# Two-layer graph network, residual and layer norm on one core: merged sums written into the PSUM tile of the sums, in pairs in the first layer

## The chip, the cores and the metric

One of the eight cores of a Trainium2 chip runs the kernel. The time is device microseconds of one execution. Four runs of the kernel before gave 2027.91, 2038.23, 2041.61 and 2043.71 us, median 2039.92 us.

## What is computed

`x` has 6250 rows (nodes) of 256 numbers. 100,000 edges go from `src` to `dst`; they are sorted by `dst`, and low-numbered nodes have many more incoming edges than high-numbered ones. In all shapes float32:

```
def _gin_agg(h, src, dst, eps, n_nodes):
    agg = jax.ops.segment_sum(h[src], dst, num_segments=n_nodes)
    return (1.0 + eps) * h + agg
...
    h = _gin_agg(x, src, dst, eps1, n)
    h = jax.nn.relu(h @ W1a + b1a)
    h = jax.nn.relu(h @ W1b + b1b)
    h = _gin_agg(h, src, dst, eps2, n)
    h = jax.nn.relu(h @ W2a + b2a)
    out = h @ W2b + b2b
...
    x = _layernorm(x + _L0_gnn_ref(x, edge_index, ...), axis=-1)
```

W1a is 256x512, W1b and W2a 512x512, W2b 512x256. So layer 1 sums rows of 256 numbers, layer 2 rows of 512.

## The kernel before, in words

The 100,000 edges make 782 chunks of 128. The first 216 chunks end at the 512 lowest nodes (the "heavy" ones); their sums are not gathered, but computed as products of a matrix of counts with all of `x` (or of the hidden `h`): 52 products a layer (line 648), added to the accumulators on VectorE (line 654). In layer 1 the counts must first be made (lines 700 to 759: VectorE's vectors `ca` and `cb`, a matmul on line 747, a copy on ScalarE, an add on VectorE).

The other 566 chunks are gathered. They fall into 94 groups of 20 to 4 chunks; the last 62 groups have 4. GpSimd issues one indirect transfer a chunk (line 505) into tiles of four chunks ("pieces"), six pieces ahead. For each group, in this order:

1. VectorE makes a selection matrix `sel` of 0 and 1 (line 517, two buffers) and a matrix `to` (line 522, three buffers) two groups ahead.
2. TensorE sums the gathered rows by 32 slots (line 854): the chunks of a group go to four parts of 32 partitions of one PSUM tile `pm`.
3. ScalarE copies `pm` to `split` in SBUF (line 872).
4. TensorE multiplies `split` by `to`, which brings the four parts' slots to their place among 128 nodes (line 877, the "unite"), into another PSUM tile `pu`.
5. VectorE adds `pu` times a mask to 3 or 4 accumulator tiles of 128 nodes (line 881).

When all adds to four accumulator tiles are done, that block of 512 nodes goes through the dense layers: transposes (line 576), two matrix products (lines 588 and 599), with copies and activations on ScalarE and VectorE. The four buffers of accumulators (line 484) are loaded on SP's queue (line 487) and scaled on ScalarE five chunks later (line 494).

The order of the instructions on each engine is written out by the loop at the end of `layer` (line 832 on); an engine works strictly in that order and waits where a value is missing. The loop issues a piece's four chunks of sums, then counts `now` up four times. At each count it issues what is due (`due`, line 533), and gives two queues a chance (`pump`): `blockwise`, the dense blocks that are ready, and `beside`, the counts and products, which earns credit at a rate set by a planner. Two queue steps or none may come between two due items. Due times: the copy comes `LAG` = 2 chunks after the group's end, the unite 1 chunk after the copy, the adds 2 after the unite.

PSUM has eight banks. Three hold the dense steps, two the counts of layer 1, and `SUMS` (3 in layer 1, 5 in layer 2) are shared by `pm`, `pu` and the products' tiles. `sum_tile` (line 547) hands them out: when all are taken, the oldest's due work is issued at once. A tile of 128x256 float32 fills half a bank, one of 128x512 a whole one.

The functions that the change touches:

Of the kernel before, what the change touches and what calls it, by code (L numbers as in the profile page):

```python
# [15 lines left out]
P = 128  # L16
# [11 lines left out]
STEP2 = 1.5  # L28
ACCS = 4
LAG = 2  # L30
SPREAD = 5.0
# [90 lines left out]
def tile_gin_residual_layernorm(  # L122
# [64 lines left out]
    srcs = const.tile([P, NCP], I32, name="srcs")  # L187
    dsti = const.tile([P, NCP], I32, name="dsti")
    dstf = const.tile([P, NCP], F32, name="dstf")
    slot = const.tile([P, NCP], F32, name="slot")  # L190
    nc.gpsimd.memset(srcs, 0)
    nc.gpsimd.memset(dsti, 0)

# [35 lines left out]
    with tc.tile_pool(name="prep", bufs=2) as prep, tc.tile_pool(  # L229
        name="prepp", bufs=2, space=bass.MemoryType.PSUM  # L230
    ) as prepp:
        full = E // P
        rest = E - full * P
# [187 lines left out]
    def ordered(ctx):  # L421
# [14 lines left out]
        for g in order:  # L436
            m = members[g]
            pieces += [(g, m[i : i + BURST]) for i in range(0, len(m), BURST)]
        first_use, last_use = {}, {}
        for k, g in enumerate(order):  # L440
# [16 lines left out]
        def layer(number, ctx, table, width, scale, wa, ba, wb, wide, prepare, finish, conclude):  # L457
# [4 lines left out]
                tc.tile_pool(name=f"psum{number}", bufs=2, space=bass.MemoryType.PSUM)  # L462
            )
            SUMS = 3 if number == 1 else 5
            acc = {}
            held = []
# [12 lines left out]
            def seed(ts):  # L479
                while len(held) >= ACCS:  # L480
                    assert blockwise.todo
                    blockwise.step()
# [30 lines left out]
            def select(g):  # L513
                c0, h = groups[g]
                n = min(PARTS * h, NCH - c0)
                sel = edge.tile([P, GRP, SLOTS], F32, tag="sel", name="sel", bufs=2)
                nc.vector.tensor_tensor(  # L517
                    sel[:, :n, :], iota[:, :SLOTS].unsqueeze(1).to_broadcast([P, n, SLOTS]),
                    slot[:, c0 : c0 + n].unsqueeze(2).to_broadcast([P, n, SLOTS]), op=ALU.is_equal,
                )  # L520
                to = edge.tile([P, P], F32, tag="to", name="to")
                nc.vector.tensor_scalar(to, iota, home[:, g : g + 1], None, op0=ALU.is_equal)  # L522
                sels[g] = sel, to
# [23 lines left out]
            def sum_tile(name):  # L547
                while len(sums_out) >= SUMS:
                    take(sums_out[0])
                pm = psum.tile([P, width], F32, tag="pm", name=name, bufs=SUMS)  # L550
                entry = [pm, None]
                sums_out.append(entry)
                return entry

            def take(entry):
                if entry in sums_out:
                    sums_out.remove(entry)
                    entry[1]()

            def take_later(entry, what):  # L560
                entry[1] = what
                later(LAG, lambda: take(entry))

# [46 lines left out]
            def products(turns, table_of):  # L610
# [28 lines left out]
                for i, (r, t) in enumerate(turns):  # L639
# [4 lines left out]
                    entry = sum_tile("pm")  # L644
                    pm = entry[0]
                    for j, k in enumerate(ks):
# [9 lines left out]

                    take_later(entry, add_product)
                    yield 0.00167 * len(ks) * width
# [126 lines left out]
            class Queue:  # L785
# [15 lines left out]
                def pump(self):  # L801
                    self.credit = min(self.credit + self.rate, 4.0)
                    if self.credit > 0:
                        self.step()

            unseeded = [b for b in blocks if b[0] >= HEAVY]
            waiting = list(blocks)
# [24 lines left out]
            for k, g in enumerate(order):  # L832
# [13 lines left out]
                beside.rate = rates[g]  # L846
                entry = sum_tile("pm")
                pm = entry[0]
                sel, to = sels.pop(g)
                parts = [[c for c, b in members[g] if b == i] for i in range(PARTS)]  # L850
                while upto < len(pieces) and pieces[upto][0] == g:
                    rows_, reads = gathered.pop(upto)
                    for j, (c, b) in enumerate(pieces[upto][1]):
                        mm = nc.tensor.matmul(  # L854
                            pm[b * SLOTS : (b + 1) * SLOTS], sel[:, c - c0, :], rows_[:, j, :],
                            start=(c == parts[b][0]), stop=(c == parts[b][-1]),
# [10 lines left out]

                def add_group(g=g, pm=pm, to=to, parts=parts):

                    split = edge.tile([P, width], F32, tag="split", name="split", bufs=2)  # L870
                    used = SLOTS * sum(1 for p in parts if p)
                    nc.scalar.copy(split[:used], pm[:used])  # L872

                    def unite():
                        entry = sum_tile("pu")
                        pu = entry[0]
                        nc.tensor.matmul(pu, to[:used], split[:used], start=True, stop=True)  # L877

                        def add():
                            for t in range(lo[g], min(hi[g], NT - 1) + 1):  # L880
                                nc.vector.scalar_tensor_tensor(  # L881
                                    acc[t], pu, mask[:, t - lo[g], g : g + 1], acc[t],
                                    op0=ALU.mult, op1=ALU.add,
                                )
# [333 lines left out]
```

## Time and profile before

| | |
|---|---|
| median of 4 runs | 2039.92 us (2027.91 to 2043.71) |
| the profiled execution | 2041.31 us |
| its span, first to last instruction | 2039.4 us |
| TensorE clock granted, mean | 0.853 of full |
| layer 1 / layer 2 in the span, about | 45 to 1007 us / 1022 to 2030 us |
| TensorE (PE) busy | 1414.3 us, 69% |
| GpSimd (POOL) busy | 1090.5 us, 53% |
| VectorE (DVE) busy | 823.0 us, 40% |
| ScalarE (ACT) busy | 372.1 us, 18% |
| DMA, mean | 165 GB/s |

How to read the profile: it shows one execution. PE is the matmuls, PEld the weight loads that run beside them. A float32 matmul appears as two rows. A group is all instructions of one line, engine and operation; `pu<-split,to` means that the tile `pu` is written from `split` and `to`. Behind `x` stands the number of instructions, behind the first bar the busy us and the mean ns of one, behind the second the idle time of the engine just before them and what ended most of it. A line of the waits has the engine, its tile and line, what it waited for, total us, times and the longest. A timeline row has the start and length in us, and in brackets the idle time before it. "issue" and "remote" say that the profile found no instruction that ended the wait.

### The profile page before, as it was taken

The page shows a single profiled execution, that of the slowest core. Times are in us where ns is not written, and L with a number is a line of the kernel's source. Part 1 is how long each engine was busy: PE and PEld are TensorE (multiplying, and loading weights), DVE is VectorE, ACT ScalarE, POOL GpSimd, SP SyncE. Part 2 cuts the span into 40 slices and gives each one's busy share as a digit, 9 for nine tenths or more (in the row PEclk, how much of TensorE's full clock was granted, in tenths as well). Part 3 has the DMA queues.
Part 4 walks back from the last instruction along what each step waited for, and adds up shares of the span by engine and source line. Part 5 has one row for each costly group of instructions (what it writes and reads, how often), then busy time and mean ns, then how long its engine had stood idle before and what let it go on. Part 6 is the DMA issues. An engine that isn't in the chain of part 4 may idle for free.

```text
span 2039.4 us, 17219 instructions
## 1 busy us (share of the span) xinstructions
PE 1414.3 (69%) x5364; PEld 622.0 (30%) x5364; DVE 823.0 (40%) x2253; ACT 372.1 (18%) x683; POOL 1090.5 (53%) x1146
## 2 busy tenths in 40 slices
PE   1244475676867867887675679585959677878777
PEld 0011132332434434433321223231314323334334
DVE  7255544444444434333211223233425366446534
ACT  0022222322222221221200001010111111111111
POOL 2766666656564465444066665646465465445420
PEclk9966687977978888997887779788969889989989
DMA  5332345545445456432297776757576486456521
GB/s 162 90 94 86 91 141 170 176 127 181 152 144 183 141 184 213 133 106 80 69 329 222 250 227 213 249 153 261 162 247 196 131 265 197 137 173 192 164 86 38
DMA packets 157811, 337.08 MB, mean 165 GB/s; under 512 B 23954, under 2 KB 70930, under 8 KB 157712
## 3 DMA queue, kind: packets, MB, share of 16 engines
q0 software_dynamic: 72448, 222.63, 36.0%
q1 hardware_dynamic: 74756, 96.90, 14.0%
q10 hardware_dynamic: 10508, 16.35, 2.3%
q8 instruction: 47, 0.77, 0.1%
q14 instruction: 52, 0.43, 0.1%
HBM read 303.75 MB, written 32.05 MB: 165 GB/s over the span
## 4 chain that ended last, share of the span: by engine, by line
PE 39%; issue 23%; another core or an unknown queue 13%; POOL 8%; DVE 6%; DMA 6%; ACT 3%; SPq 1%; DVEq 0%; ACTq 0%; POOLq 0%
PE po L599 10%; PE ph L588 10%; POOL g L505 8%; PE pm L648 8%; PE pm L854 6%; PE pu L877 3%; DVE acc L881 3%; DMA r<-in_x_dram 2%; DMA acc<-h 2%; PE pt L576 1%; PE pc L747 1%; DMA g<-h,srcs 1%; ACT split L872 1%; DMA g<-in_x_dram,srcs 1%
## 5 line engine op out<-in xcount | busy, mean ns | idle before, releaser
L505 POOL DMA_INDIRECT g<-h,srcs x566 | 537.0, 949 | 473.0 <-issue 216.6
L505 POOL DMA_INDIRECT g<-in_x_dram,srcs x566 | 550.0, 972 | 370.3 <-issue 149.0
L881 DVE SCALAR_TENSOR_TENSOR acc<-pu,mask,acc 128x256 f32<-128x256 f32 (+1 forms) x666 | 365.1, 607 | 103.4 <-PE pu L877 47.0
L877 PE MATMUL pu<-split,to 128*128 128x256 f32 (+2 forms) x376 | 192.3, 598 | 220.9 <-ACT split L872 146.1
L648 PE MATMUL pm<-xr,cf 128*128 128x256 f32 (+3 forms) x784 | 308.8, 541 | 49.3 <-issue 29.9
L854 PE MATMUL pm<-g,sel 128*32 128x256 f32 (+1 forms) x2264 | 279.5, 561 | 81.3 <-issue 31.1
L648 PEld LDWEIGHTS pm<-xr,cf 128*128 128x128 f32 (+1 forms) x784 | 164.4, 217 | 208.5 <-issue 160.8
L654 DVE TENSOR_TENSOR acc<-pm,acc 128x256 f32<-128x256 f32 (+1 forms) x104 | 57.7, 555 | 410.0 <-remote 198.8
L747 PE MATMUL pc<-cb,ca 128*128 128x490 f16 x216 | 89.1, 485 | 146.7 <-DVE cb L708 37.3
L588 PE MATMUL ph<-zt,w2a_s 128*128 128x512 f32 (+1 forms) x416 | 184.1, 596 | 5.2 <-ACT zt L579 5.2
L599 PE MATMUL po<-w1b_s,ht 128*128 128x512 f32 (+1 forms) x392 | 174.0, 595 | 0.0
L877 PEld LDWEIGHTS pu<-split,to 128*128 128x128 f32 (+1 forms) x376 | 71.4, 219 | 321.6 <-ACT split L872 178.9
L872 ACT COPY split<-pm 128x256 f32<-128x256 f32 (+2 forms) x188 | 88.1, 479 | 394.4 <-remote 209.6
L854 PEld LDWEIGHTS pm<-g,sel 128*32 128x32 f32 x2264 | 51.7, 116 | 284.4 <-issue 225.1
L738 ACT CAST cs<-pc 128x490 f16<-128x490 f32 x151 | 84.5, 570 | 245.3 <-remote 129.3
L517 DVE TENSOR_TENSOR sel<-iota,slot 128x128 f32<-128x128 f32 (+5 forms) x188 | 65.5, 349 | 137.0 <-remote 78.3
L588 PE MATMUL ph<-zt,w1a_s 128*128 128x512 f32 (+1 forms) x208 | 105.9, 648 | 21.5 <-issue 12.0
L588 PEld LDWEIGHTS ph<-zt,w2a_s 128*128 128x128 f32 x416 | 79.4, 203 | 112.7 <-issue 89.0
L704 DVE TENSOR_SCALAR ca<-wide,low 128x128 f16<-128x128 f16 x216 | 59.5, 275 | 125.6 <-remote 79.1
L522 DVE TENSOR_SCALAR to<-iota,home 128x128 f32<-128x128 f32 x188 | 57.4, 305 | 111.4 <-PE pu L877 64.9
L576 PE MATMUL pt<-ident,acc 128*128 128x128 f32 (+1 forms) x294 | 56.5, 335 | 65.5 <-issue 51.2
L599 PEld LDWEIGHTS po<-w1b_s,ht 128*128 128x128 f32 (+1 forms) x392 | 73.4, 189 | 88.0 <-issue 86.7
(104 smaller groups left out, 828.6 us busy)
## 6 DMA issues: line engine op xcount, KB each, us to landing
xr<-in_x_dram SPq DMA_DIRECT2D x48, 512.0 KB
h<-h1r ACTq DMA_DIRECT2D x48, 256.0 KB
counts<-cf SPq DMA_DIRECT2D x48, 256.0 KB
acc<-h SPq DMA_DIRECT2D x12, 1024.0 KB
xr<-h SPq DMA_DIRECT2D x12, 1024.0 KB
cf<-counts SPq DMA_DIRECT2D x48, 256.0 KB
g<-in_x_dram,srcs POOLq DMA_INDIRECT x566
g<-h,srcs POOLq DMA_INDIRECT x566
```

Of the source, the lines that this page charges most:

```text
L505: nc.gpsimd.indirect_dma_start(out=tile_[:, j, :], out_offset=None, in_=table, in_offset=bass.IndirectOffsetOnAxis(ap=srcs[:, c : c + 1], ...
L517: nc.vector.tensor_tensor(sel[:, :n, :], iota[:, :SLOTS].unsqueeze(1).to_broadcast([P, n, SLOTS]), slot[:, c0 : c0 + n].unsqueeze(2).to_br ...
L576: nc.tensor.transpose(pt[:, k, :m], a[:m, k * P : (k + 1) * P], ident[:m, :m])
L588: nc.tensor.matmul(ph[:, :nb], wa[:, k, f * P : (f + 1) * P], zt[:, k, :nb], start=(k == 0), stop=(k == kk - 1),)
L599: nc.tensor.matmul(po[:m], ht[:, f, i * P : i * P + m], wb[:, f, :], start=(f == 0), stop=(f == KH - 1),)
L648: nc.tensor.matmul(pm, cf[:m, j, :], xr[:m, j, :], start=(j == 0), stop=(j == len(ks) - 1),)
L738: nc.scalar.copy(cs, pc)
L747: mm = nc.tensor.matmul(pc, a, b, start=(i == 0), stop=(i == len(pair) - 1))
L854: mm = nc.tensor.matmul(pm[b * SLOTS : (b + 1) * SLOTS], sel[:, c - c0, :], rows_[:, j, :], start=(c == parts[b][0]), stop=(c == parts[b][ ...
L872: nc.scalar.copy(split[:used], pm[:used])
L877: nc.tensor.matmul(pu, to[:used], split[:used], start=True, stop=True)
L881: nc.vector.scalar_tensor_tensor(acc[t], pu, mask[:, t - lo[g], g : g + 1], acc[t], op0=ALU.mult, op1=ALU.add,)
```

## The change

`pu` is gone: the unite writes into the tile that held the group's sums. In layer 1 two groups share a tile (`BATCH` = 512 // width = 2), so one copy serves two groups; layer 2 keeps one group a tile. The copy, the unites and the adds of a tile are a list, taken one after the other, each two chunks after the one before (`LAGS`). A tile is given back after its last list entry. `to` gets six buffers. `dsti`, needed only at the start, moves to a pool that is closed after it. The last group always has a tile of its own. In `seed`, what is due is issued if no dense step is left to do.

```diff
+LAGS = (2, 2, 2)
...
-    dsti = const.tile([P, NCP], I32, name="dsti")
...
-    nc.gpsimd.memset(dsti, 0)
...
+        dsti = prep.tile([P, NCP], I32, tag="dsti", name="dsti", bufs=1)
+        nc.gpsimd.memset(dsti, 0)
...
+        def batched(n):
+
+            rest = order[:-1]
+            return [rest[i : i + n] for i in range(0, len(rest), n)] + [order[-1:]]
+
...
+            BATCH = 512 // width
             SUMS = 3 if number == 1 else 5
+            batch_of = {g: b for b in batched(BATCH) for g in b}
...
                 while len(held) >= ACCS:
+                    if not blockwise.todo:
+                        due(all=True)
                     assert blockwise.todo
                     blockwise.step()
...
-                to = edge.tile([P, P], F32, tag="to", name="to")
+                to = edge.tile([P, P], F32, tag="to", name="to", bufs=6)
...
             def sum_tile(name):
                 while len(sums_out) >= SUMS:
-                    take(sums_out[0])
-                pm = psum.tile([P, width], F32, tag="pm", name=name, bufs=SUMS)
-                entry = [pm, None]
+                    oldest = sums_out[0]
+                    assert oldest[1]
+                    while oldest[1]:
+                        take(oldest, len(oldest[1]))
+                pm = psum.tile([P, BATCH, width], F32, tag="pm", name=name, bufs=SUMS)
+                entry = [pm, []]
                 sums_out.append(entry)
                 return entry
 
-            def take(entry):
-                if entry in sums_out:
-                    sums_out.remove(entry)
-                    entry[1]()
-
-            def take_later(entry, what):
-                entry[1] = what
-                later(LAG, lambda: take(entry))
+            def take(entry, left_over):
+
+                if len(entry[1]) == left_over:
+                    entry[1].pop(0)[1]()
+                    if entry[1]:
+                        take_later(entry)
+                    else:
+                        sums_out.remove(entry)
+
+            def take_later(entry):
+                n = len(entry[1])
+                later(entry[1][0][0], lambda: take(entry, n))
...
-                    take_later(entry, add_product)
+                    entry[1].append((LAG, add_product))
+                    take_later(entry)
...
+            def add_batch(pm, of):
+
+                n = len(of)
+                used = max(u for g, to, u in of)
+                split = None
+
+                def copy():
+                    nonlocal split
+                    split = edge.tile([P, BATCH, width], F32, tag="split", name="split", bufs=2)
+                    nc.scalar.copy(split[:used, :n, :], pm[:used, :n, :])
+
+                def unite():
+                    for i, (g, to, u) in enumerate(of):
+                        nc.tensor.matmul(pm[:, i, :], to[:u], split[:u, i, :], start=True, stop=True)
+
+                def add():
+                    for i, (g, to, u) in enumerate(of):
+                        for t in range(lo[g], min(hi[g], NT - 1) + 1):
+                            nc.vector.scalar_tensor_tensor(
+                                acc[t], pm[:, i, :], mask[:, t - lo[g], g : g + 1], acc[t],
+                                op0=ALU.mult, op1=ALU.add,
+                            )
+                            uses[t] -= 1
+
+                return list(zip(LAGS, (copy, unite, add)))
...
-                entry = sum_tile("pm")
+                batch = batch_of[g]
+                if g == batch[0]:
+                    entry = sum_tile("pm")
+                    members_to = []
                 pm = entry[0]
+                at = batch.index(g)
...
-                            pm[b * SLOTS : (b + 1) * SLOTS], sel[:, c - c0, :], rows_[:, j, :],
+                            pm[b * SLOTS : (b + 1) * SLOTS, at, :],
+                            sel[:, c - c0, :], rows_[:, j, :],
...
-                def add_group(g=g, pm=pm, to=to, parts=parts):
-
-                    split = edge.tile([P, width], F32, tag="split", name="split", bufs=2)
-                    used = SLOTS * sum(1 for p in parts if p)
-                    nc.scalar.copy(split[:used], pm[:used])
-
-                    def unite():
-                        entry = sum_tile("pu")
-                        pu = entry[0]
-                        nc.tensor.matmul(pu, to[:used], split[:used], start=True, stop=True)
-
-                        def add():
-                            for t in range(lo[g], min(hi[g], NT - 1) + 1):
-                                nc.vector.scalar_tensor_tensor(
-                                    acc[t], pu, mask[:, t - lo[g], g : g + 1], acc[t],
-                                    op0=ALU.mult, op1=ALU.add,
-                                )
-                                uses[t] -= 1
-
-                        take_later(entry, add)
-
-                    later(1, unite)
-
-                take_later(entry, add_group)
+                members_to.append((g, to, SLOTS * sum(1 for p in parts if p)))
+                if g == batch[-1]:
+                    entry[1] += add_batch(pm, members_to)
+                    take_later(entry)
```

More of the change, by code (lines that the diff above doesn't have):

```diff
@@ L644, in products @@
                     entry = sum_tile("pm")
-                    pm = entry[0]
+                    pm = entry[0][:, 0, :]
                     for j, k in enumerate(ks):
```

## The prediction, made before the changed kernel was run

> **What bounds the kernel now.** I read the busy times first, then the waits of TensorE and of GpSimd, then the groups by shape, then the timeline where the waits are long.
>
> ```profile
> PE 1414.3 (69%) x5364; PEld 622.0 (30%) x5364; DVE 823.0 (40%) x2253; ACT 372.1 (18%) x683; POOL 1090.5 (53%) x1146
> ```
>
> No engine is full. PE has the most work and is idle for 2039.4 - 1414.3 = 625 us. GpSimd, which issues the gathers, comes second, so its waits say who leads:
>
> ```profile
> POOL g L505 <- issue: 365.7, 968, 68.2
> POOL g L505 <- PE pm L854: 303.8, 62, 11.6
> ```
>
> The columns are total us, times, longest. 62 long waits end when PE has used up a gathered tile: gathers run ahead of PE, six pieces deep, and stop for PE. So PE's chain sets the pace, and what counts is what PE stands idle for:
>
> ```profile
> PE pu L877 <- ACT split L872: 146.1, 40, 22.4
> PE pm L648 <- DVE acc L881: 13.2, 10, 3.6
> PE pm L854 <- ACT split L872: 9.1, 2, 7.1
> ```
>
> The largest single entry is the merging matmul (the "unite" on line 877) waiting for ScalarE's copy of the sums. The groups by shape give all idle time before it, whatever the releaser (the number behind the second bar):
>
> ```profile
> L877 PE MATMUL pu<-split,to 128*128 128x512 f32 x186 | 115.8, 709 | 152.0 <-ACT split L872 97.4 <-issue 27.2 <-ACT acc L494 15.4
> L877 PE MATMUL pu<-split,to 128*128 128x256 f32 x186 | 74.6, 489 | 66.9 <-ACT split L872 46.6 <-issue 10.7 <-DVE acc L881 5.2
> ```
>
> So 66.9 us in layer 1 (width 256), 152.0 us in layer 2 (width 512), 1.9 us more for the two short last groups: 220.9 us, a third of PE's idle time. This is what the change is aimed at.
>
> But not all of it is the copy. Going through the timeline unite by unite, 21 of the 188 stand over 3 us and hold 160.6 us (8 with 40.1 us in layer 1, 13 with 120.5 us in layer 2); the copy itself takes 0.373 us (128x256) or 0.585 us (128x512). The timeline shows what a long stop is made of:
>
> ```profile
> 639.89 1.99 PE L648 MATMUL pm<-xr,cf 128*128 128x256 f32 x8 [0.58 <-DVE acc L881]
> ...
> 644.83 0.29 DVE L517 TENSOR_TENSOR sel<-iota,slot 128x128 f32<-128x128 f32 x1 [4.14 <-remote]
> 644.89 0.37 ACT L872 COPY split<-pm 128x256 f32<-128x256 f32 x1 [3.88 <-remote]
> ...
> 645.31 0.64 PE L854 MATMUL pm<-g,sel 128*32 128x256 f32 x8 [3.43 <-issue]
> ```
>
> PE's last product is over at 641.9 by its row, yet VectorE's next selection and ScalarE's copy, both readers of sums that PE made before 641.9, start together at 644.8. They got PE's signal late, and PE then waited for them. In such a stop every reader of PE waits, the copy is only one of them, and whatever PE would do next (here the next group's sums, which also need a selection) stops just the same.
>
> The Trainium skill bears on this and speaks against the change: "Perfetto Trace Analysis", section Tensor Engine Instruction, says that a matmul's end in a profile is an estimate, and that the signal follows the real write, outside the row. By it the long waits before the unite are PE's own late finish and no distance after the copy removes them; only the short waits count. The rows above point the same way, and the sum below is worked out both ways from rows alone.
>
> **The change, part by part.** I walked the counter `now`, the due list and the two queues' credits through the loop, once by the old lines and once by the new, to see how many other PE steps (a burst of sums, a product, a dense step, a count) are issued between a group's copy and its unite.
>
> *Copy to unite: one chunk becomes two.* Old, layer 1: 39 unites with nothing between, 51 with one step, 4 with two; their idle times by the timeline sum to 34.9, 32.6 and 0.2 us, so 0.89, 0.64 and 0.05 us each. Layer 2: 63, 30 and 1, with 109.7, 43.5 and 0 us, so 1.74, 1.45 and 0. New, layer 2: 50, 23 and 21. At the old means that is 50 x 1.74 + 23 x 1.45 = 120.4 us instead of 153.2, 32.8 less.
>
> *Two groups per tile in layer 1.* 94 waits become 48, as the second unite of a pair follows the first: 11 with nothing between, 24 with one step, 13 with more: 11 x 0.89 + 24 x 0.64 + 13 x 0.05 = 25.8 us instead of 67.7, 41.9 less. Together 74.7 us, if long waits shrink like short ones. If long ones stay whole, only 27.6 us (layer 1) and 32.7 us (layer 2) of short waits are at stake, and the same shares give 27.6 x 41.9 / 67.7 + 32.7 x 32.8 / 153.2 = 17.1 + 7.0 = **24.1 us**. I take this lower one, because the timeline above shows the next step waiting for the same late signal. Ends: 0 and 220.9 us.
>
> *Sums in the same PSUM tile.* The old code takes two tiles per group (`pm`, then `pu`) out of 3 in layer 1; the new takes one per two groups, but holds it until the adds. By the walk, a full list forced an early copy 11 times in layer 1 before and never after; layer 2 (5 tiles) has one such case in both. So the stops of PE for a tile go in layer 1: products waiting for adds 13.2 us less 4.6 us in layer 2 (the waits in that window), and sums waiting for the copy 9.1 us: **17.7 us** less. Ends: 0, and 22.3 us for both layers.
>
> The skill has a rule against this part: "PSUM — Partial Sum Buffer", section "Summary: rules for kernel authors", says to evacuate PSUM promptly. By that rule the longer hold would cost new tile stops; by the walk the list is never full in layer 1, so I charge none.
>
> *Copies.* 93 copies of 0.373 us become 47 of about 0.585 us (the 128x512 row): 34.7 to 27.5 us of ScalarE, which is 18% busy. Nothing on the path.
>
> *Adds later and in pairs.* Adds come 6 chunks after the group's end instead of 5, and in layer 1 after the end of the pair's second group. 333 adds a layer over 94 groups are 3.54 a group, 0.474 us each in layer 1: a pair runs 7 adds, 3.36 us, where 1.68 us ran before. VectorE (40% busy) hides it where nobody behind is due. Behind it stand the next selections, which the sums need one group later, the products' adds, and the count's vectors. The transposes of a finished block wait for the last add: 12 blocks x 1.68 us = 20 us at most; I take a quarter, **5 us**, as in most blocks another queue step is at hand. Ends: 0 and the price of rival C.
>
> *`to` with 6 buffers.* VectorE stood 64.9 us at line 522 for an older unite. That goes, but the adds behind it wait for the same unite, so I count nothing; if it helped, it would be in VectorE's own waits, at most 64.9 us.
>
> *`dsti` in the other pool.* Its memset (0.75 us) moves behind GpSimd's other start work, which ends at 3.0 us; VectorE first writes `dsti` at 7.96 us. Nothing, up to 0.75 us.
>
> *What does not move.* The walk gives the same `now` for all 13 loads of accumulator tiles in both layers, the same gathers, the same DMAs: no queue (SP, GpSimd, ScalarE's) gets another order of transfers. Dense blocks become ready 1 chunk later in layer 2 and 0 to 9 in layer 1; no load was forced to wait for a block before, none is after. At the end the last group is alone in its tile and is drained in one go, as before.
>
> Sum: -24.1 - 17.7 + 5 = -36.8 us. The profiled execution took 2041.31 us (span 2039.4), so 2004.5; the median of the four runs, 2039.92, would give 2003. I say **2004 us**.
>
> **Rivals.**
>
> *A, the long waits shrink too.* -74.7 - 17.7 + 5 = -87.4: **1954 us**. For it: PE has real work to do in the added distance (21 unites of layer 2 get two steps where 1 had). Against: the 644.8 rows.
>
> *B, PE waits elsewhere for the same signal.* The unite's waits go and come back before the sums (selection late) or the transposes: **2040 us**, within 10 us. For it: the wait at 645.31 is already not at a unite. This is also how it looks if the change does not do what it says, which the walk speaks against.
>
> *C, slower: VectorE's bunches stop PE.* Place: layer 1, where each pair's 7 adds stand ahead of the count's vectors (lines 704 and 708), for which PE already waits 36.5 + 37.3 us, and of the block's last add. Price: 1.68 us for each of 46 pairs that lands on PE, against 41.8 us won. It breaks even at 25 pairs, is slower by 0.5% (10 us) from 31, and at 40 pairs gives 67.2 - 41.8 = +25: **2066 us**. Against: the bunch comes half as often, and the selections are one group ahead.
>
> **How the numbers follow.** The forecast 0.42, A 0.20, B 0.16, C 0.22. Half a per cent, 10 us, is about what a measurement of this kernel can tell from no change. So faster 0.62, same 0.16, slower 0.22. Range: down to 1930, past A because the unite's idle could go further than the class means say (its end is 220.9 us), and up to C's 2066. The forecast and A alone span 1930 to 2030.
>
> **What would show it.** Right: idle before unites near 25 us plus the long waits in layer 1, some 128 us and more in layer 2; no PE wait of line 854 for a copy; 48 copies of layer 1 at about 0.585 us; GpSimd waiting longer for PE in fewer steps. A: idle before layer 2's unites near 120 us or less and the clock above 0.853. B: the same PE idle of 625 us, more of it before the sums and the transposes. C: longer waits at lines 747 and 576 for adds. Wrong altogether if PE's late signals themselves come more or less often: I do not know what makes them, and a change of their number by a tenth of the idle time is 60 us.

## The result, and the profile after

The changed kernel takes 2046.99 us (median of 50 runs, 2029.98 to 2069.29), the kernel before beside it 2037.29 us (76 runs). The ratio is 1.0049, 95% interval 1.0034 to 1.0064: a little slower, where 2004 us was forecast. The ratios in this document are over fast runs alone and the medians over all runs, so that a ratio can differ from the quotient of two medians by up to 0.3%. The profiled execution of the changed kernel took 2045.51 us, its span 2043.7 us.

The busy times of the kernel after. TensorE has 10 us more work in rows than before, and its idle time, 2043.7 - 1424.3 = 619.4 us, is 6 us less: nearly nothing was gained where 37 us were expected.

```profile
PE 1424.3 (70%) x5364; PEld 624.7 (31%) x5364; DVE 821.7 (40%) x2253; ACT 368.6 (18%) x637; POOL 1094.1 (54%) x1146
```

The groups by shape of the kernel after (idle before them behind the second bar), the unites of each layer and the count's matmul:

```profile
L837 PE MATMUL pm<-split,to 128*128 128x512 f32 x186 | 115.0, 705 | 117.4 <-issue 52.8 <-ACT split L833 51.6 <-DMA g<-h,srcs 9.3
...
L765 PE MATMUL pc<-cb,ca 128*128 128x490 f16 x216 | 86.5, 473 | 205.2 <-DVE ca L722 68.5 <-ACT cs L756 61.2 <-issue 25.2
L837 PE MATMUL pm<-split,to 128*128 128x256 f32 x186 | 60.7, 459 | 23.7 <-ACT split L833 13.6 <-issue 9.3 <-ACT cf L746 0.8
```

The unites did what the class means of the prediction said: with the two short groups of each layer, 153.2 us became 118.6 in layer 2 and 67.7 became 24.5 in layer 1 (120.4 and 25.8 were worked out). But the count's matmul, which had 146.7 us of idle before it in the kernel before,

```profile
L747 PE MATMUL pc<-cb,ca 128*128 128x490 f16 x216 | 89.1, 485 | 146.7 <-DVE cb L708 37.3
```

has 205.2 now. The waits of TensorE and GpSimd after (total us, times, longest) name what it waits for; the entry of the sums for a copy (9.1 us before) is gone, as foreseen, and GpSimd still waits for TensorE:

```profile
PE pc L765 <- DVE ca L722: 68.5, 14, 23.7
PE pm L837 <- ACT split L833: 67.2, 13, 18.2
PE pm L837 <- issue: 62.1, 15, 11.4
PE pc L765 <- ACT cs L756: 61.2, 12, 14.4
```

```profile
POOL g L515 <- issue: 370.8, 973, 72.8
POOL g L515 <- PE pm L902: 317.7, 72, 10.3
```

Split at the start of layer 2's first gather, the two layers went opposite ways. The table adds up TensorE's idle time by the step that follows it (start-up left out), in us, for the profiles that the text uses. "Late" and "prompt" chips are explained with the experiments.

| | before | after | after, 3rd (e12) | by layer (e13) | no unites (e15) | before, prompt chip (e11) | after, prompt chip (e8) |
|---|---|---|---|---|---|---|---|
| layer 2's first gather at | 1016.9 | 1047.3 | 1046.0 | 1007.0 | 1022.1 | 839.9 | 845.7 |
| layer 2, from there to the end | 1022.5 | 996.4 | 1006.6 | 1004.6 | 976.1 | 856.5 | 857.1 |
| idle, layer 1 | 326.6 | 360.5 | 353.7 | 327.8 | 369.4 | 185.9 | 194.3 |
| of it before unites | 67.7 | 24.5 | 28.0 | 36.7 | 0 | 19.2 | 12.6 |
| before counts | 146.7 | 205.2 | 170.8 | 163.2 | 209.4 | 43.3 | 48.1 |
| before sums | 63.3 | 56.3 | 62.0 | 47.3 | 79.4 | 109.8 | 117.9 |
| idle, layer 2 | 263.8 | 222.8 | 235.6 | 230.7 | 257.4 | 131.7 | 127.6 |
| of it before unites | 153.2 | 118.6 | 129.5 | 115.1 | 0 | 51.9 | 42.4 |

Layer 2 gained 26 us. In layer 1 the unites lost 43 us of idle time and all other steps together won 77, so that layer 1 is 30 us longer. In this pair of profiles the change is two effects of opposite sign, 26 and 30 us. Each column is one execution, and the sizes are uncertain: layer 2 is the same program in the columns after, 3rd and e13 and in e1 below, and took 996.4, 1006.6, 1004.6 and 1009.7 us.

### The profile page after: what moved, and what is told of

It is laid out like the page before. It is cut to its first block, busy times and chain, and to the rows that moved or that the text cites. A ratio compares the mean times of both kernels' runs of the same rounds, so it can differ in the third digit from the quotient of the medians.

```text
span 2043.7 us, 17133 instructions
## 1 busy us (share of the span) xinstructions
PE 1424.3 (70%) x5364; PEld 624.7 (31%) x5364; DVE 821.7 (40%) x2253; ACT 368.6 (18%) x637; POOL 1094.1 (54%) x1146
## 4 chain that ended last, share of the span: by engine, by line
PE 45%; another core or an unknown queue 18%; issue 14%; DVE 8%; POOL 6%; DMA 5%; ACT 3%; DVEq 0%; ACTq 0%; SPq 0%; POOLq 0%
PE ph L605 11%; PE po L616 11%; PE pm L665 9%; POOL g L515 6%; PE pm L902 6%; PE pm L837 5%; DMA g<-h,srcs 1%; DVE acc L842 1%; PE pt L593 1%; PE pc L765 1%; DVE at L740 1%; DVE cb L726 1%; DVE ca L722 1%; ACT zt L596 1%
## 5 line engine op out<-in xcount | busy, mean ns | idle before, releaser
L842 DVE SCALAR_TENSOR_TENSOR acc<-pm,mask,acc 128x256 f32<-128x256 f32 (+1 forms) x666 | 361.3, 607 | 203.0 <-PE pm L837 76.6
L665 PE MATMUL pm<-xr,cf 128*128 128x256 f32 (+3 forms) x784 | 315.6, 550 | 55.5 <-issue 32.7
L837 PE MATMUL pm<-split,to 128*128 128x256 f32 (+2 forms) x376 | 177.6, 581 | 143.1 <-ACT split L833 67.2
L765 PE MATMUL pc<-cb,ca 128*128 128x490 f16 x216 | 86.5, 473 | 205.2 <-DVE ca L722 68.5
L605 PE MATMUL ph<-zt,w2a_s 128*128 128x512 f32 (+1 forms) x416 | 194.5, 621 | 35.2 <-issue 22.8
L833 ACT COPY split<-pm 128x512 f32<-128x512 f32 (+1 forms) x142 | 81.9, 581 | 407.2 <-remote 240.3
L837 PEld LDWEIGHTS pm<-split,to 128*128 128x128 f32 (+1 forms) x376 | 76.5, 220 | 223.5 <-issue 121.5
L936 DVE TENSOR_TENSOR h1t<-po,b1b_s 128x512 f32<-128x512 f32 (+1 forms) x49 | 33.9, 691 | 179.1 <-PE po L616 158.8
L740 DVE TENSOR_TENSOR at<-cs,at 128x490 f16 x151 | 77.9, 516 | 66.2 <-ACT cs L756 47.5
```

Source lines behind the costliest of these rows:

```text
L605: nc.tensor.matmul(ph[:, :nb], wa[:, k, f * P : (f + 1) * P], zt[:, k, :nb], start=(k == 0), stop=(k == kk - 1),)
L665: nc.tensor.matmul(pm, cf[:m, j, :], xr[:m, j, :], start=(j == 0), stop=(j == len(ks) - 1),)
L740: nc.vector.tensor_tensor(to, cs.rearrange("p (k w) -> p k w", w=W), to, op=ALU.add)
L765: mm = nc.tensor.matmul(pc, a, b, start=(i == 0), stop=(i == len(pair) - 1))
L833: nc.scalar.copy(split[:used, :n, :], pm[:used, :n, :])
L837: nc.tensor.matmul(pm[:, i, :], to[:u], split[:u, i, :], start=True, stop=True)
```

## Experiments

The theories. **P**: the pairs bunch VectorE's adds. **S**, later **L**: TensorE's late signals set the pace, and idle time that is taken from the unites comes back elsewhere. **F**: in layer 1 the unite one chunk behind its copy filled the time in which the next count waits, and two chunks behind it leaves that wait bare. A fourth one, that the later adds cost, came up before the fifth series. "Distance" is that from copy to unite. The ratios are against the kernel before on the same chip, with 95% intervals. The first and fourth series ran on one "late" chip each, the second and fifth on one "prompt" chip, the third on another prompt one; the words are explained in the third. On which chip the first result was taken is not on record; its profiles look like those of the late chips.

**First series: the parts apart.** e1 is the changed kernel without pairs, e2 with distance 1, e3 the kernel before with distance 2.

```diff
e1  -            BATCH = 512 // width
e1  +            BATCH = 1
e2  -LAGS = (2, 2, 2)
e2  +LAGS = (2, 1, 2)
e3  -                    later(1, unite)
e3  +                    later(2, unite)
```

> One group a tile in layer 1 too (the distances stay 2, 2, 2). In the profile of the changed kernel layer 1 ended 30 us later than before and layer 2 took 26 us less. Theory P (pairs): the pairs are what holds layer 1, by longer bunches on VectorE and later copies ahead of the count; then the idle time before the count's matmul falls from 205 us to about 150 us, layer 2's first gather comes at about 1017 to 1025 us instead of 1047, and the ratio to the kernel before is 0.985 to 0.992. Theory S (signal): PE's idle time is set by how late its signals come, and goes wherever PE next waits; then the ratio is 0.998 to 1.010 and PE's idle time stays within 20 us of 620. Against both, the walk gives 23 early drains of a full tile list in layer 1, at perhaps 1 us each.

> The unite again one chunk after the copy, the pairs of layer 1 kept. Theory P: layer 2 loses its gain (idle before its unites back from 119 us to about 150 us) and layer 1 stays slow: ratio 1.010 to 1.020. Theory S: the idle time before the unites rises, the rest falls by as much: ratio 1.000 to 1.008.

> The kernel before with the one number changed: the unite two chunks after the copy, still into a tile of its own. Theory P: both layers gain what the class means gave (layer 2: 33 us of idle before unites): ratio 0.980 to 0.990. Theory S: idle before the unites falls by 20 to 40 us a layer and comes back before counts, sums and transposes: ratio 0.996 to 1.006.

Measured: e1 2045.3 us, 1.0106 (1.0060 to 1.0151); e2 2032.38 us, 1.0019 (0.9979 to 1.0059); e3 2032.13 us, 1.0036 (0.9995 to 1.0077); before 2029.61 us. Taking the pairs away does not make it faster, so P falls (in e1's one profile layer 1 is 20 us shorter than after the change, 1027.1 us, and layer 2, the same program, 13 us longer). Shared tile and pairs at the old distance (e2) are worth nothing here. S had e2 and e3 inside its ranges and e1 just above. e3 has the pattern of the change without its tiles: layer 2's first gather at 1037.0 us, 20 us behind the first profile and 24 behind e2, and 982.7 us from there to the end.

**Second series: distance by layer, and two probes.** These ran on another chip, on which the kernel before took 1703.04 us, not 2030. `number` is the layer.

```diff
e5  -                return list(zip(LAGS, (copy, unite, add)))
e5  +                return list(zip((2, number, 2), (copy, unite, add)))
e6  -                    later(1, unite)
e6  +                    later(number, unite)
```

e4b is the changed kernel without copies and unites (the adds read the sums), e7 the kernel before with each matmul of the sums issued twice.

> The changed kernel with the distance from copy to unite set by layer: 1 chunk in layer 1, 2 in layer 2. In the profiles so far layer 2's first gather came at 1013 and 1017 us with distance 1 and at 1027, 1037 and 1047 us with distance 2; PE's idle time in layer 2 was 248 and 264 us with distance 1 and 212 to 237 us with 2. Theory F (filler): in layer 1 the unite, one chunk behind the copy, fills the time in which the count's next matmul waits for its vectors and its copy; moved on, it leaves that wait bare. In layer 2 there are no counts, and the distance pays. Then ratio 0.985 to 0.993, layer 2's first gather at about 1015 us. Theory S (late signals, idle time conserved): 0.998 to 1.006.

> The kernel before with distance 2 in layer 2 alone (tile of its own for the unite, no pairs). Theory F: the same gain as the changed kernel by layers, ratio 0.985 to 0.993, PE idle in layer 2 about 215 us instead of 264. Theory S: 0.998 to 1.004.

> Left out of the computation, from the changed kernel: the copy and the unite; the adds read the sums as they are. It takes away 178 us of PE's busy time and the 143 us of idle time before it, and 82 us of ScalarE. If those waits were what the time consists of, it falls by about 320 us, to about 1725 us. Theory S: the idle time returns before other steps and only PE's busy share goes: 1860 to 1900 us. If another chain sets the pace, it falls by less than 100 us.

> The kernel before with every matmul of the sums issued twice, so that the gathered sums are doubled: about 280 us more of PE by its rows. If PE's idle time is slack that it spends waiting for others, part of the work falls into it: less than 200 us more. If PE is really occupied longer than its rows say, and the sums are what keeps it (the late signals came mostly behind them), it costs more than its rows: over 350 us.

Measured: e5 1690.13 us, 0.9915 (0.9886 to 0.9943); e6 1701.39 us, 0.9975 (0.9956 to 0.9994); e4b 1644.33 us, 0.9648 (0.9611 to 0.9684); e7 1772.47 us, 1.0400 (1.0360 to 1.0439). Distance 1 in layer 1 and 2 in layer 2 is faster, as F said; e6 gains less than F asked. The expectation of e4b was written for a kernel of 2040 us; against 1703 us it falls by 59 us. e7 puts 1132 matmuls (2264 rows) more on TensorE, whose busy time is 1498.6 us (1342.6 in e11 below, on the other prompt chip), and only 69 us on the time: on this chip much of TensorE's idle time is slack into which work can fall.

**Third series: the same with a base on one chip.** e8 is the changed kernel, e9 is e5 again, e11 the kernel before, profiled; e10 has distance 2 in layer 1 alone.

```diff
e10 -                    later(1, unite)
e10 +                    later(2 if number == 1 else 1, unite)
```

> The changed kernel once more, beside three others on one chip; if it is the chip on which the kernel before takes 1703 us, its profile there is new. In the trace of before at 2039.4 us, 58 of TensorE's stops, 380 us together, are such that TensorE's own signals come over 0.8 us after the ends of their rows; in the traces at 1644 to 1770 us there is no such stop. Theory L (these late signals set the pace, and distance only chooses the row before which the stop shows): where they are present after stands at 1.000 to 1.010 of before; where they are absent nothing takes the gain back, and after is at least as good as the version with distance 1 in layer 1, 0.985 to 0.993 of before. Theory F (in layer 1 the unite one chunk behind its copy fills the time in which the next count waits for ca, cb and its PSUM copy; two chunks on, that wait is bare): layer 1 loses 10 to 30 us against distance 1 on any chip, so where before takes 1703 us after is at 0.997 to 1.010, with over 70 us of TensorE idle before the count's row (51 us with distance 1).

> The changed kernel with the unite one chunk behind its copy in layer 1 and two in layer 2, which stood at 0.9915 (0.9886 to 0.9943) of before where that takes 1703 us. Theory F: faster than before on either kind of chip, 0.983 to 0.995, and faster than the changed kernel by 10 to 30 us. Theory L: 0.988 to 0.994 where before takes about 1700 us, as the changed kernel does; where before takes about 2035 us, 0.997 to 1.005, since the idle that leaves the unites comes back.

> The kernel before with the unite two chunks behind its copy in layer 1 alone: the distance alone, in the layer that grew by 30 us, with nothing of the tiles or the pairs changed. Theory F: 1.005 to 1.015, and the idle before the count's row up by 10 us or more. Theory L: 0.997 to 1.004, and the idle before the count's row up by no more than the idle before the unites falls. Together with the distance in layer 2 alone (0.9975, 0.9956 to 0.9994, where before takes 1703 us) it should give the distance in both.

> The kernel before, unchanged, profiled once more on the chip of the other three, so that their idle time by step has a base of the same chip. Ratio 1.000. Theory L: where its time is about 1700 us, no stop of TensorE with signals later than 0.8 us after the rows, and some 300 us of idle in place of 590; where it is about 2035 us, 50 to 65 such stops with 350 to 420 us, at the same places of the program as in the first trace. Theory F says nothing of it.

Before took 1706.76 us. Measured: e8 1697.84 us, 0.9952 (0.9934 to 0.9970), so on this chip the change makes the kernel a little **faster**; e9 1693.84 us, 0.9925 (0.9900 to 0.9950); e10 1711.98 us, 1.0028 (1.0011 to 1.0046); e11, one run, 1698.31 us. The effects add up: tiles and pairs about -0.5% (e9 less e6; -0.6% by e5), layer 2's distance -0.25%, layer 1's +0.28%, together -0.5%. The series fits neither theory well: e8 lies in neither range (F from 0.997, L up to 0.993), e9 is 4 us faster than e8 where F asked 10 to 30, e10 lies in L's range, and the idle before the count's row in e8, 48.1 us, is not the over 70 us that F asked for.

What sets these chips apart is in the waits of TensorE. On e11, the unchanged kernel:

```profile
PE pm L854 <- DMA g<-in_x_dram,srcs: 92.2, 41, 4.9
PE pu L877 <- ACT split L872: 69.1, 40, 12.6
PE pc L747 <- DVE cb L708: 32.3, 14, 23.6
PE pm L854 <- DMA g<-h,srcs: 31.8, 9, 6.2
```

TensorE waits 124 us for gathered data (17 us in the first profile), and 69 us for copies where it was 146. And the signals: counting for each recorded signal of TensorE how long after the last row's end it comes, before has 293 of 1090 over 0.5 us, after 303 of 1066, e1 to e3 much the same; e11 has 2 of 1301, e8 2 of 1248. So there are late chips and prompt chips. The kernel, its instructions and its transfers are the same on both. The late signals are not the whole difference: of the 343 us between the two spans, 271 us are TensorE's idle time (625 against 354) and 72 us are longer rows, at a granted clock of 0.853 against 0.917.

**Fourth series: on a late chip.** e12 is the changed kernel, e13 is e5, e15 is e4b once more; e14 halves the gathers.

```diff
e14 -                    for j, (c, b) in enumerate(pieces[i][1])
e14 +                    for j, (c, b) in enumerate(pieces[i][1]) if j % 2 == 0
...
e14 -                            pm[b * SLOTS : (b + 1) * SLOTS], sel[:, c - c0, :], rows_[:, j, :],
e14 +                            pm[b * SLOTS : (b + 1) * SLOTS], sel[:, c - c0, :], rows_[:, j // 2 * 2, :],
```

> The changed kernel a third time, as the base of the others. Where TensorE's signals come late: 1.002 to 1.008 of before by theory L and by theory F. Where they don't: 0.993 to 0.998, as in the run on the other such chip (0.9952).

> The changed kernel with distance 1 in layer 1 and 2 in layer 2. Where the signals come late: theory L 0.998 to 1.003 (idle conserved); theory F 0.985 to 0.995, since layer 1 keeps the pace of distance 1 (1013 to 1017 us to the first gather of layer 2) and layer 2 that of distance 2 (983 to 997 us). Where they don't: 0.989 to 0.995 by both.

> The kernel before with every second gathered chunk not gathered: its matmul reads the rows of the chunk ahead of it, so half of the 1132 gathers and their bytes are left out. If late signals go with the traffic of the gathers, the signals late by over 0.5 us fall from about 290 to below 150 and the time by 150 us or more; if not, they stay above 250 and the time within 50 us. Where no signal is late: the idle before the sums, 152 us, which ends with the gathers' data, falls to some 60 us, and the time to 0.93 to 0.96 of before.

> The changed kernel without copies and unites (the adds take the sums unmerged; that part of the computation is left out). Where the signals come late: theory L: the 143 us of idle before the unites go to other rows, and only the 178 us of the unites' own rows can be gained, 0.92 to 0.96 of before; against it, if the idle belongs to the way from sums over copy to unite, 178 and 143 us go, 0.83 to 0.87. Where they don't: 0.961 to 0.969, as on the other such chip.

Before took 2033.77 us. Measured: e12 2042.52 us, 1.0021 (0.9995 to 1.0048); **e13 2016.78 us, 0.9907 (0.9875 to 0.9940)**; e14 1539.52 us, 0.7560 (0.7524 to 0.7596); e15 1997.45 us, 0.9809 (0.9770 to 0.9848).

e13 beats both kernels on a late chip too, and what it has over e12 is layer 1 alone: its first gather of layer 2 comes 39 us earlier, the rest is 2 us shorter. So L was wrong on this: idle time does not always come back, and unite and adds one chunk later in layer 1 cost 25.7 us by the medians (2042.52 - 2016.78), 1.1% by the ratios, 41 us between the two profiled executions.

e15 lies above both ranges (0.92 to 0.96, 0.83 to 0.87), on L's side. The waits before unites and the unites' own rows, 157.5 and 183.8 us in e12, are gone, and with them only 45 us against e12, 36 us (1.9%) against the kernel before. Two things took the rest (the two profiled executions differ by 54 us). The idle time before all other steps is 195 us more than in e12: the sums, the counts and the dense steps now wait, as L says. And the other rows take 92 us more, at a granted clock of 0.799 against 0.846; no theory had that, and what lowers the clock is not shown. The busy times of e12 and of e15:

```profile
PE 1427.5 (70%) x5364; PEld 626.1 (31%) x5364; DVE 822.4 (40%) x2253; ACT 369.2 (18%) x637; POOL 1096.8 (53%) x1146
```

```profile
PE 1335.3 (67%) x4988; PEld 564.6 (28%) x4988; DVE 815.2 (41%) x2253; ACT 294.9 (15%) x495; POOL 1092.1 (55%) x1146
```

On prompt chips e4b gained 3.0% over the changed kernel (0.9648 against 0.9952), some 52 us, where e8 has 224 us of unites and waits before them; there too the other rows are 80 us longer, at a clock of 0.877 against 0.914. The groups of e15:

```profile
L899 PE MATMUL pm<-g,sel 128*32 128x256 f32 (+1 forms) x2264 | 316.6, 588 | 181.4 <-issue 76.1 <-DVE sel L527 45.8 <-DMA g<-h,srcs 13.7
L605 PE MATMUL ph<-zt,w2a_s 128*128 128x512 f32 (+1 forms) x416 | 198.8, 636 | 61.2 <-ACT zt L596 48.1 <-issue 10.1 <-ACT ht L609 3.1
...
L765 PE MATMUL pc<-cb,ca 128*128 128x490 f16 x216 | 89.5, 492 | 209.4 <-ACT cs L756 82.2 <-DVE ca L722 53.7 <-DVE cb L726 38.1
```

e14, half the gathers, has 33 of 1139 signals late by over 0.5 us, and this is its page:

```profile
PE 1302.0 (85%) x5364; PEld 579.1 (38%) x5364; DVE 816.5 (53%) x2253; ACT 370.3 (24%) x683; POOL 556.0 (36%) x580
...
PEclk9988999999999999999799999999999999999899
```

TensorE's work is the same 5364 matmul rows, 85% busy, with most slices at nine tenths of the clock (the digits; 0.956 in the mean), and 494 us have gone. Against the first profile 112 us are saved in shorter rows and 395 us in idle time. So the late signals nearly vanish with half of the gathers. Their bytes went too (225.7 MB are moved in place of 337.1), so gathers and traffic are not told apart, and neither is enough by itself: on a prompt chip the full gathers leave no late signals.

**Fifth series: what in layer 1 costs.** This is the chip of the second series. Copy, unite and adds come in layer 1 (2, 4, 6) chunks behind the sums in the changed kernel, (2, 3, 5) in e13. Layer 2 is as changed in all three.

```diff
     -                return list(zip(LAGS, (copy, unite, add)))
e16  +                return list(zip(((1, 2, 2) if number == 1 else (2, 2, 2)), (copy, unite, add)))
e17  +                return list(zip(((2, 1, 3) if number == 1 else (2, 2, 2)), (copy, unite, add)))
e18  +                return list(zip(((2, 2, 1) if number == 1 else (2, 2, 2)), (copy, unite, add)))
```

> The changed kernel with copy, unite and adds of layer 1 at 1, 3 and 5 chunks behind the sums (the changed kernel 2, 4 and 6; the version that is faster 2, 3 and 5); layer 2 as changed. If the place of the unite or of the adds is what costs layer 1: as the faster version or better, 0.985 to 0.993 of before. If the two chunks between copy and unite themselves cost, by whatever way: 1.000 to 1.006 where TensorE's signals come late, 0.994 to 0.998 where they don't.

> Layer 1 with copy, unite and adds at 2, 3 and 6 chunks: the unite where the faster version has it, the adds where the changed kernel has them. Theory of the unite's place on TensorE: 0.987 to 0.994. Theory of the adds (their place on VectorE, the tiles held longer): 1.000 to 1.006 where TensorE's signals come late, 0.994 to 0.998 where they don't.

> Layer 1 with copy, unite and adds at 2, 4 and 5 chunks: the unite where the changed kernel has it, the adds where the faster version has them, one chunk behind the unite. Theory of the unite's place on TensorE: 1.000 to 1.006 where TensorE's signals come late, 0.994 to 0.998 where they don't. Theory of the adds: 0.987 to 0.994.

A prompt chip, before 1707.63 us. Measured: e16 1690.06 us, 0.9906 (0.9876 to 0.9935); e17 1708.86 us, 1.0000 (0.9975 to 1.0026); e18 1687.47 us, 0.9889 (0.9858 to 0.9919). The unite in the changed kernel's place with adds at five chunks (e18) is the fastest; the unite at the early place with adds at six (e17) has lost everything and is slower than either theory had it. e17 and e18 differ in two things, so the runs are best read in pairs, with e5 of the second series (same chip) and e8 (the other prompt chip):

| layer 1 on prompt chips | adds at 5 | adds at 6 |
|---|---|---|
| unite at 3 | 0.9915 (e5) | 1.0000 (e17) |
| unite at 4 | 0.9889 (e18) | 0.9952 (e8) |

The adds one chunk later cost 0.85% (e5 to e17, one chip) or 0.6% (e18 to e8, two chips). The unite one chunk later does not cost; it gains 0.3% or 0.5%, the smaller of which is within the intervals. Both together cost about 0.3% (e8 against e9, e10). The copy's place makes no difference that can be told (e16 against e5). F falls: it is not the unite's place or its distance from the copy that costs layer 1 on these chips, but the **adds**, six chunks behind the sums in place of five. On late chips e16 to e18 were not run; there the 25.7 us stand for unite and adds together, and that they are the adds is argued from the prompt chips, not shown.

One trace of the late adds is in VectorE's own waits, of e17 and then of e18 (the count's add of `cs` to `at`, which waits for ScalarE's copy of the count):

```profile
DVE at L740 <- ACT cs L756: 36.1, 11, 5.7
```

```profile
DVE at L740 <- ACT cs L756: 22.5, 9, 4.7
```

Over all profiles this wait tells the two groups apart. With adds at five chunks: 15.0, 12.5 and 23.7 us on late chips (before, e2, e13), 21.9 to 29.2 on prompt ones (e11, e5, e6, e9, e16, e18). With adds at six: 47.5, 54.1, 46.3 and 29.3 on late chips (after, e12, e3, e1), 34.0 to 36.1 on prompt ones (e8, e10, e17). It marks the group but does not measure the loss: e1, the slowest against its base, has the lowest value with adds at six, and TensorE's idle time before counts is 50.3 us in e17 and 48.8 in e18.

Walking the loop's counter through e18 and the changed kernel, which differ in nothing but this, gives what moves in layer 1: 325 adds by one chunk, of which 37 fall behind one of 5 steps of the count's vectors on VectorE; and, since a dense block starts when its last add is issued, the transposes and both products of 36 of the 49 tiles by one chunk on TensorE. The order in the two traces confirms the 37 adds, and has the transposes of 16 tiles behind some other step of TensorE. No run separates the two, but the traces limit the first: e17 is 8.4 us behind e5 at the last matmul of the counts (603.6 against 595.2 us) and 17.5 us behind at the last sums of layer 1; e8 is 3.9 us behind e9 at the first point and 10.7 at the second. So half of the loss or more comes where no count is left, and the waits of the count's add can be only a part of it. That the rest is the dense blocks is likely, not shown.

## Why the prediction was wrong, step by step

**The bound.** TensorE's chain, with GpSimd waiting for it, was right for the profile that was read. But 380 of the 625 us of idle time lie in stops with late signals, and these nearly vanish with half of the gathers (e14).

**Copy to unite, -24.1 us.** The mechanism held: the idle time before unites fell. The size was too small: 77.8 us less, where the class means gave 74.7 and the choice for short waits 24.1. Counted as the prediction counted, the short waits (3 us or less) fell by 46 us, from 60.2 to 14.0, and not by 24. The long ones of layer 2 stayed as the prediction said (13 with 120.6 us before, 14 with 113.5 after); those of layer 1, where pairs halve the number of waits, fell (8 with 40.1 us, 2 with 15.6). For layer 2 it was worth something on the way to the end: -7.0 us was taken, -26 us is the difference of the two profiles; e13 against e2 (0.9907 and 1.0019, on two late chips) gives 1.1%, some 23 us. There rival A was nearer. On a prompt chip the same step gives 0.25% (e6).

**Same PSUM tile, -17.7 us.** The waits went, as the walk of the loop said: products waiting for adds fell from 13.2 to 1.9 us, sums waiting for copies from 9.1 us to none. But TensorE's whole idle time before sums and products rose, from 130.5 to 146.0 us in the two layers: it waits there for something else. And e2, which has tiles and pairs without the distance, is at 1.0019 (0.9979 to 1.0059): nothing gained on a late chip, about 0.5% on prompt ones (e5 and e9 against e6). So this term was not there on the chip of the forecast.

**Adds later and in pairs, +5 us.** This is the step that failed. It priced the pairs' bunch at a block's last add and took a quarter of 20 us, "as in most blocks another queue step is at hand"; that with the adds the dense blocks become ready later ("1 chunk later in layer 2 and 0 to 9 in layer 1") stood under "What does not move", at no price. On prompt chips the adds one chunk later cost 0.85% (e5 to e17) or 0.6% (e18 to e8), some 11 to 15 us. On a late chip they were moved only together with the unite, and the two cost 25.7 us (e12 and e13, one chip), where the prediction had -17.1 us for copy to unite and pairs, and +5. The pairs are not shown to be the harm: without them it is not faster (e1). So rival C had VectorE and the dense blocks' last adds, but put the price on the size of the bunch; what the runs show is a price on how late the adds come. Why unite and adds together cost 25.7 us there and some 5 us on prompt chips (e10) stays open.

**The sum.** By the two profiles. Predicted for layer 1: -17.1 - 17.7 + 5 = -29.8 us; the profiles show +30.4. Predicted for layer 2: -7.0; the profiles show -26.1. Together +4.3 where -36.8 was forecast. That the total came out near nothing is chance: two effects several times as large happen to be of opposite sign.

**Rival B** came nearest (2040 us within 10), for a reason that is half its own: in layer 1 the idle did turn up before other steps, mostly before the counts (146.7 to 205.2 us) and only 12 us of it before the transposes that it named; in layer 2 it did not come back. e15 shows how far B's rule holds: take the unites away altogether, and of 341 us 45 are gained, though longer rows have a share of 92 us in that.

**Long waits and late ends.** The prediction set the Trainium skill's page "Perfetto Trace Analysis", section Tensor Engine Instruction, beside the late rows: a matmul's end in a profile is estimated, and the signal follows the real write. In the prompt profiles there is next to no difference: 2 signals of 1248 in e8 come over 0.1 us after a row's end. On late chips 303 of 1066 in the kernel after come over 0.5 us behind. From that rule the prediction concluded that a distance can't remove long waits. For layer 2 the counts above agree; in layer 1 they fell by 24.5 us, with half as many waits. What the rule could not tell is where a stop that leaves the unites turns up.

## What to carry to other kernels

When a step is moved back, follow what is released by it as far as the next queue: here, on the prompt chips, the harm was not in the unite that moved, but in the adds behind it, with which the dense blocks start. Idle time before a step is what that step happens to meet, not what its removal is worth; test each stage of a change apart, since one knob (`LAGS`) may have opposite signs in two layers. Set by layer, or with the adds drawn forward again, the same idea is faster than both kernels: 0.9907 on a late chip (e13), 0.9889 on a prompt one (e18).

## What the hardware showed unexpectedly

The same kernel takes about 2030 us on the two late chips and about 1705 us on the two prompt ones, with the same instructions, bytes (337 MB) and GpSimd time (1090.5 and 1093.0 us). Most of the difference is idle time of TensorE around late signals. The timeline of the kernel after (start, length, and in brackets the idle time before):

```profile
1105.80 3.17 PE L665 MATMUL pm<-xr,cf 128*128 128x512 f32 x7
...
1115.97 0.69 DVE L671 TENSOR_TENSOR acc<-pm,acc 128x512 f32<-128x512 f32 x1 [25.48 <-issue]
...
1120.14 0.95 POOL L515 DMA_INDIRECT g<-h,srcs  x1 [0.30 <-issue]
1126.51 0.58 ACT L833 COPY split<-pm 128x512 f32<-128x512 f32 x1 [41.37 <-remote]
1126.52 0.69 DVE L527 TENSOR_TENSOR sel<-iota,slot 128x512 f32<-128x512 f32 x1 [9.85 <-remote]
1126.75 1.28 POOL L515 DMA_INDIRECT g<-h,srcs  x1 [5.67 <-remote]
...
1127.15 2.08 PE L837 MATMUL pm<-split,to 128*128 128x512 f32 x2 [18.19 <-ACT split L833]
```

The last product's row ends at 1108.97. The product's add on VectorE starts 7 us later, and ScalarE, VectorE and GpSimd, three readers of TensorE, all start within 0.24 us at 1126.5, 17.5 us after TensorE's last row. Until 1121 GpSimd issues a gather every 1.25 us without a break. The same product and its add in e8, on a prompt chip, under gathers of the same rate:

```profile
899.58 3.70 PE L665 MATMUL pm<-xr,cf 128*128 128x512 f32 x8
...
903.32 0.69 DVE L671 TENSOR_TENSOR acc<-pm,acc 128x512 f32<-128x512 f32 x1 [4.49 <-PE pm L665]
```

Here the add starts 0.04 us after the row. On the late chips there are 55 to 61 stops of over 2.5 us with such signals in each profile, 380 us together before, 423 after, 387 without unites, and 3 with 20 us at half the gathers; on the prompt chips, in the profiles of e8, e11 and e18, there are none. Within one stop, late signals that are more than 0.3 us apart are a whole multiple of 0.71 us apart (in the kernel before, 1 to 25 times that; 31 of 36 within 0.1 of a whole number); the rest of a bunch follow about 0.04 us apart. What holds them back, whether the signal is late or the row itself, and why two of these four chips do it, stays open.
